# Causal attention with a gated sign network: half of the probability transposes by VectorE and SBUF-to-SBUF transfers, and the values' products ahead of the scores

## The chip, the cores and the metric

The kernel runs on one core of a Trainium2 chip. The metric is device microseconds of one execution, from start to end. The program is written with named engines: PE (TensorE, matmuls), DVE (VectorE), ACT (ScalarE), POOL (GpSimd) and SP (SyncE, which here only issues DMAs). Everything is fp32.

## The reference

```python
# x: (4, 512, 1024)
m = jnp.mean(x, -1, keepdims=True); v = jnp.var(x, -1, keepdims=True)
xn = (x - m) / jnp.sqrt(v + eps)
# attention, 16 heads of 64, rotary on q and k, causal
q, k, v = (split_heads(xn @ W) for W in (Wq, Wk, Wv))
p = softmax(mask(rotary(q) @ rotary(k).T / 8))
s = merge_heads(p @ v) @ Wo
# gate: a network with the signs of its weights and per-token channel scales
r = softmax(xn @ gate_w.T)                   # 8 experts
y = (xn * (r @ in_scale)) @ sign(weight).T
g = silu(y * (r @ out_scale) + bias)
return x + s * g
```

The listing is abridged. What matters for the change is the product of the softmax's probabilities with the values. The scores of a 512 x 512 head lie with queries on partitions, so that the row maximum and sum run along the free dimension. The product with V needs keys on partitions. So every probability block of 128 x 128 that the causal mask leaves (10 of 16 per head) must be transposed in between: 4 batches x 16 heads x 10 = 640 blocks.

## The kernel before, in words

**Units, groups, slots.** A *unit* `(b, g, i)` is a pair of heads, 2 x 64 rows on 128 partitions. A *group* `(b, g)` is two units, four heads; there are 16 groups. The main loop (from L879) has one *slot* per group. In the slot of group k, PE computes the projections of group k. Three weight blocks (q, k and a half of v's) make 84 steps, most of them one step of a Strassen scheme with matmuls of 128 x 256 (`project_qk` L330, matmul L342; `project_v` L410, matmul L429). Among these steps lie the attention *pieces* of groups before: scores of group k-1 and values of group k-2, which are called the "late" units, `w` (unit 0) and `v` (unit 1).

**The order.** PE's order is written by hand: `manual_schedule(engines={PE})` (L70) makes PE run in program order. `attention_pieces` (L839) gives a list of closures, and `interleave` (L870) spreads the projection steps evenly behind them. The other engines are ordered by the framework's scheduler, which moves instructions among each other as it expects them to become ready, except those wrapped in `keep_in_program_order`. The built program's order on each engine is fixed before the run.

**The pieces before.** Sixteen of them: five banks of transposes of `w`; block 1's scores of both units and `values(w)`; five banks of transposes of `v`; block 3's scores of both units and `values(v)`; nothing; blocks 2 and 0 of both units (`scores_02`); nothing; nothing. Some slots add to these: the router (`router` L617, a new batch's routing matmuls), loads, the sign weights, and in the slots with g > 1 the next batch's layernorm (`layernorm` L198, which is called ahead of the slot's pieces, L914 and L915) and the transposes of its normalized x (`transpose_x`).

**Scores.** `scores` (L512) takes a list of blocks. Block i is 128 queries of two heads against the (i+1) x 128 keys that the mask leaves. It has two matmuls on PE (L517), mask add and row maximum on DVE (L528, L532), two exponentials with row sums on ACT (L535), the reciprocal on DVE (L543) and two scalings on POOL (L545), in place in the probability tile. The scores lie in PSUM in the pool `ps_sc`: two buffers of two banks each. A buffer is free for PE again once the exponentials have read it. Probability tiles were three tags in the pool `probs`: block 1 (3 buffers), block 3 (2), blocks 0 and 2 together (2).

**Transposes.** `transpose_p` (L577) puts up to four 128 x 128 transposes by PE (L583) into one bank of the four-bank PSUM `ring`, which the projections use too, and copies the bank into the tile `pT` (one buffer), by DVE (L587) or by ACT (L589) in turn. `values` (L591) runs eight matmuls (L599) from `pT` into one bank, copies the result over V's tile by DVE (L608) and stores it to the HBM array `at_d` (L609, SP's queue).

**Other work that the prediction's steps name.** `form_w` (L296) and `form_x` are DVE's sums of Strassen's quarters of the weights and of x. `rotary` has four ACT copies of 32 partitions (L323, L324), one DVE product and two POOL operations (L326, L327) per unit and per q or k. Weight loads are SP DMAs of 1 MB, issued by `load_w` (L245) for a pool of three buffers. `rt_d` takes the router's result, 16 KB per store.

**The tail.** After the last slot come the last group's scores, three units' transposes and values, the gate (`dense` takes steps of the sign network's matmuls as fill) and the output projection. Before, the order from L1058 is: transposes of `w`, `split(0, 0)`, `scores_1`, `split(0, 1)`, `values(w)`, then transposes of `v` with `dense` between them, `scores_3`, `values(v)`, `dense`, ..., `scores_02`.

Of the kernel before, what the change touches and what calls it, by code (L numbers as in the profile page):

```python
# [21 lines left out]
H, D = 16, 64  # L22
# [13 lines left out]

T_BANKS = [
    [(0, 0, i) for i in range(4)],
    [(1, 0, i) for i in range(4)],
    [(0, 1, 1), (0, 1, 2), (0, 1, 3), (0, 3, 3)],  # L40
    [(1, 1, 1), (1, 1, 2), (1, 1, 3), (1, 3, 3)],
    [(0, 2, 2), (0, 2, 3), (1, 2, 2), (1, 2, 3)],
]


def t_place(h, j):

    return [(h, 0), (2 + h, 0), (4, 256 * h), (2 + h, 384)][j]
# [3 lines left out]
def attn_gated_ffn_kernel(  # L52
# [453 lines left out]
    def probs(u, i):  # L506

        if i % 2:
            return PR[u, i]
        return PR[u, 0][:, :, P * i // 2 : P * i // 2 + (i + 1) * P]  # L510
# [42 lines left out]
    def new_probs(u, n, cols, bufs):  # L553
        PR[u, n] = pp.tile(
            [P, 2, cols], F32, tag=f"p{n}", name="p%d_%d_%d_%d" % (n, *u), bufs=bufs
        )

    def scores_1(units):
        ps = sc_bank(units[0], 1)
        for u in units:  # L560
            new_probs(u, 1, 2 * P, 3)
        scores([(u, 1, ps[:, :, n * TH : (n + 1) * TH]) for n, u in enumerate(units)])

    def scores_3(units):
        for u in units:
            new_probs(u, 3, S, 2)
        scores([(u, 3, sc_bank(u, 3)) for u in units])

    def scores_02(units):
        blocks = []  # L570
        for u in units:
            new_probs(u, 0, S, 2)
            ps = sc_bank(u, 0)
            blocks += [(u, 2, ps[:, :, P:]), (u, 0, ps[:, :, :P])]
        scores(blocks)

    def transpose_p(u, n):  # L577
        un = "%d_%d_%d" % u
        if u not in PT:
            PT[u] = ptp.tile([P, 5, S], F32, tag="pT", name=f"pT_{un}")  # L580
        tp = tp_bank(f"ptp_{un}_{n}")
        for k, (h, j, i) in enumerate(T_BANKS[n]):
            nc.tensor.transpose(tp[:, k, :], probs(u, i)[:, h, j * P : (j + 1) * P], ident)  # L583
        dst = PT[u][:, n, :]
        src = tp.rearrange("p j q -> p (j q)")
        if n % 2:
            nc.vector.tensor_copy(dst, src)  # L587
        else:
            nc.scalar.copy(dst, src)  # L589

    def values(u):  # L591
        b, g, i = u
        pr = g + NGRP * i
        pv = bank("pv_%d_%d_%d" % u)
        for j in range(TPB):
            for h in range(2):
                r = h * D
                n, o = t_place(h, j)
                nc.tensor.matmul(  # L599
                    pv[r : r + D, j * P :],  # L600
                    lhsT=V[u][:, j, r : r + D],
                    rhs=PT[u][:, n, o : o + (TPB - j) * P],
# [4 lines left out]
        at = V[u].rearrange("p t c -> p (t c)")  # L607
        nc.vector.tensor_copy(at, pv)  # L608
        nc.sync.dma_start(  # L609
            out=at_d[b].rearrange("t p (c q) -> p t c q", c=NC)[:, :, pr, :],  # L610
            in_=at.rearrange("p (t q) -> p t q", t=TPB),
# [227 lines left out]
    def attention_pieces(k, late):  # L839
# [4 lines left out]
        def pt(u):  # L844
            return [lambda n=n: transpose_p(u, n) for n in range(5)] if u else []

        def with_values(scores_of, u):
            def both():
                scores_of(units)
                if u:  # L850
                    values(u)

            return both

        def wait():
            pass

        pieces = [
            *pt(w),
            with_values(scores_1, w),  # L860
            *pt(v),
            with_values(scores_3, v),
            wait,
            lambda: scores_02(units),
            wait,
            wait,
        ]
# [11 lines left out]
    for k, (b, g) in enumerate(groups):  # L879
# [4 lines left out]
        if g == 0:  # L884
# [14 lines left out]
            else:  # L899

                if b < B - 1:
                    pieces.insert(7, routing[0])
                pieces.insert(10, routing[1])
# [518 lines left out]
```

## Time and profile before

| | |
|---|---|
| median of 3 runs | 1169.93 us (1169.38 to 1170.2) |
| profiled execution, its own time | 1170.42 us |
| its span, first to last instruction | 1168.6 us |
| mean granted TensorE clock | 0.998 |
| PE busy (matmul) | 1159.0 us, 99%, 5816 instructions |
| DVE busy | 826.0 us, 71%, 1452 instructions |
| ACT busy | 496.8 us, 43%, 1132 instructions |
| POOL busy | 559.8 us, 48%, 590 instructions |
| DMA | 121.92 MB, mean 104 GB/s |

All of this comes from one profiled execution. Its own time is 1.8 us above its span: the rest lies before the first and after the last instruction. A group of instructions is written with its line, its engine, output <- input by the program's names and the tile's size; then a count, busy time, mean duration, and the idle time of the engine just before these instructions with the one that ended it. Matmuls are pipelined: one starts before the other has ended, so that busy sums and means of PE say less than the distance from start to start. In the order in time, each line gives the start in us, the duration, the engine, the line and the operation; several alike are joined to one line with their count. A bracket at the end tells an idle time before and who ended it.

A batch of four slots takes some 209 us, so a slot some 52 us, and DVE is busy 34 to 41 us of each.

### The profile page before, as it was taken

What the parts mean: (1) busy time and instruction counts of PE and PEld (TensorE: products, weight loads), DVE (VectorE), ACT (ScalarE), POOL (GpSimd) and SP (SyncE); (2) the same over time, 40 slices, a digit from 0 to 9 for tenths busy, and PEclk for the clock granted to TensorE, in tenths of its full rate; (3) what the DMA queues carried; (4) which work ended last, traced back from release to release, by engine and by line L of the source; (5) the groups of instructions that cost most, each with busy time, mean ns of one, the idle gap of its engine ahead of it and who ended that gap; (6) DMA issues with size and microseconds to landing.
All of it is one profiled execution on the core that took longest, in us unless ns stands there. A gap on an engine that the chain in (4) does not pass through costs nothing.

```text
span 1168.6 us, 16127 instructions
## 1 busy us (share of the span) xinstructions
PE 1159.0 (99%) x5816; PEld 851.2 (73%) x5816; DVE 826.0 (71%) x1452; ACT 496.8 (43%) x1132; POOL 559.8 (48%) x590
## 2 busy tenths in 40 slices
PE   9999999999999999999999999999999999999998
PEld 8887787878778787877878787877775455545554
DVE  7866686677767667776867776675768786677664
ACT  2552664354356444534743563364442131223121
POOL 0661554355246435623642654264465554454435
PEclk9999999999999999999999999999999999999999
DMA  8412522322242141223236221220603424332331
GB/s 311 134 37 90 162 82 67 133 84 82 81 132 103 54 153 50 98 100 118 81 91 226 84 73 58 78 82 14 216 15 108 130 95 145 112 95 100 135 108 54
DMA packets 62319, 121.92 MB, mean 104 GB/s; under 512 B 5280, under 2 KB 40864, under 8 KB 56224
## 3 DMA queue, kind: packets, MB, share of 16 engines
q1 hardware_dynamic: 57376, 112.11, 28.6%
q0 software_dynamic: 4576, 8.39, 2.1%
q8 instruction: 46, 0.75, 0.2%
q10 hardware_dynamic: 288, 0.39, 0.1%
q14 instruction: 33, 0.27, 0.1%
HBM read 95.45 MB, written 25.43 MB: 103 GB/s over the span
## 4 chain that ended last, share of the span: by engine, by line
PE 92%; DVE 3%; ACT 2%; issue 1%; POOL 1%; POOLq 0%; DVEq 0%; ACTq 0%
PE pj L342 31%; PE wo L1243 15%; PE pj L429 15%; PE ff L1183 7%; PE pv L599 6%; PE sc L517 6%; PE ptp L583 6%; PE ff L1004 3%; PE xtp L210 1%; ACT p L535 1%; PE idle L793 1%; DVE S L296 1%; PE lg L622 1%; DVE w L296 1%; ACT sw L324 1%
## 5 line engine op out<-in xcount | busy, mean ns | idle before, releaser
L545 POOL TENSOR_SCALAR p<-p,rs 128x128 f32<-128x128 f32 (+3 forms) x256 | 171.2, 682 | 265.6 <-DVE rs L543 265.5
L535 ACT ACTIVATE p<-sc,nmx 128x128 f32<-128x128 f32 (+3 forms) x256 | 132.7, 524 | 158.9 <-DVE nmx L532 151.4
L342 PE MATMUL pj<-X,w 128*128 128x256 f32 x576 | 138.3, 381 | 0.2 <-ACT X L216 0.2
L326 POOL TENSOR_TENSOR sw<-sw,sin_sb 128x512 f32<-128x512 f32 x64 | 87.5, 1367 | 94.8 <-ACT sw L324 79.0
L342 PE MATMUL pj<-T,S 128*128 128x256 f32 x512 | 123.4, 382 | 0.1
L342 PEld LDWEIGHTS pj<-X,w 128*128 128x128 f32 x576 | 105.1, 190 | 14.4 <-issue 1.8
L342 PE MATMUL pj<-T,w 128*128 128x256 f32 x448 | 107.6, 381 | 0.0
L589 ACT COPY pT<-ptp 128x512 f32<-128x512 f32 x96 | 56.2, 586 | 120.3 <-PE ptp L583 119.9
L532 DVE TENSOR_REDUCE nmx<-sc 128x2 f32<-128x512 f32 (+3 forms) x128 | 103.7, 821 | 2.9
L342 PEld LDWEIGHTS pj<-T,S 128*128 128x128 f32 x512 | 93.3, 190 | 13.0 <-issue 0.4
L429 PE MATMUL pj<-w,X 128*128 128x256 f32 x416 | 99.6, 386 | 2.6 <-DVE w L296 2.6
L327 POOL TENSOR_TENSOR rot<-rot,sw 128x512 f32<-128x512 f32 x64 | 93.7, 1464 | 4.7
L583 PE MATMUL ptp<-ident,p 128*128 128x128 f32 x640 | 94.8, 273 | 0.3 <-ACT pT L589 0.3
L323 ACT ACTIVATE sw<-c 32x512 f32<-32x512 f32 x128 | 80.4, 628 | 34.6 <-DVE c L356 32.6
L583 PEld LDWEIGHTS ptp<-ident,p 128*128 128x128 f32 x640 | 79.0, 141 | 16.5 <-DVE pT L587 0.9
L342 PEld LDWEIGHTS pj<-T,w 128*128 128x128 f32 x448 | 82.1, 190 | 11.4 <-issue 1.8
L429 PEld LDWEIGHTS pj<-w,X 128*128 128x128 f32 x416 | 77.7, 193 | 14.0 <-DVE w L296 3.0
L517 PE MATMUL sc<-rot,rot 64*128 64x384 f32 (+3 forms) x512 | 82.0, 449 | 0.0
L429 PE MATMUL pj<-w,T 128*128 128x256 f32 x352 | 81.8, 383 | 0.0
L324 ACT ACTIVATE sw<-c 32x512 f32<-32x512 f32 x128 | 80.4, 628 | 1.7
L599 PE MATMUL pv<-pT,v 128*64 128x256 f32 (+3 forms) x512 | 76.0, 439 | 0.0
L528 DVE TENSOR_TENSOR sc<-sc,mask 128x256 f32<-128x256 f32 x128 | 53.8, 420 | 28.7 <-PE sc L517 28.4
(180 smaller groups left out, 2086.5 us busy)
## 6 DMA issues: line engine op xcount, KB each, us to landing
w<-in_wqk SPq DMA_DIRECT2D x31, 1024.0 KB, 5.2
w<-in_wv SPq DMA_DIRECT2D x16, 1024.0 KB, 4.8
x<-in_x SPq DMA_DIRECT2D x16, 512.0 KB, 3.7
xn_d<-X SPq DMA_DIRECT2D x16, 512.0 KB, 5.8
at_d<-v SPq DMA_DIRECT2D x32, 256.0 KB, 2.3
xp<-xn_d SPq DMA_DIRECT2D x16, 512.0 KB, 4.8
ap<-at_d SPq DMA_DIRECT2D x16, 512.0 KB, 4.9
xr<-in_x SPq DMA_DIRECT2D x32, 256.0 KB, 2.8
```

The source lines that it names most:

```text
L324: nc.scalar.activation(sw[r + 32 : r + 64, :], c[r : r + 32, :], AF.Copy, scale=sc)
L326: nc.gpsimd.tensor_tensor(sw, sw, sin_sb, op=ALU.mult)
L327: nc.gpsimd.tensor_tensor(rot, rot, sw, op=ALU.add)
L342: nc.tensor.matmul(ps, lhsT=wq[:, k, :], rhs=xq[:, k, :], start=(k == 0), stop=(k == 3))
L429: nc.tensor.matmul(ps[:, j, :], lhsT=xq[:, k, j * P : (j + 1) * P], rhs=wq[:, k, :], start=(k == 0), stop=(k == 3),)
L517: nc.tensor.matmul(ps[:, h, :], lhsT=Q[u][r : r + D, i * P : (i + 1) * P], rhs=K[u][r : r + D, : (i + 1) * P], start=True, stop=True,)
L532: nc.vector.tensor_reduce(nmx, ps, AX.X, ALU.max, negate=True)
L535: nc.scalar.activation(pt[:, h, :], ps[:, h, :], AF.Exp, bias=nmx[:, h : h + 1], accum_out=ssum[:, h : h + 1],)
L545: nc.gpsimd.tensor_scalar(pt[:, h, :], pt[:, h, :], rs[:, h : h + 1], 1.0, op0=ALU.mult, op1=ALU.mult,)
L583: nc.tensor.transpose(tp[:, k, :], probs(u, i)[:, h, j * P : (j + 1) * P], ident)
L599: nc.tensor.matmul(pv[r : r + D, j * P :], lhsT=V[u][:, j, r : r + D], rhs=PT[u][:, n, o : o + (TPB - j) * P], start=(j == 0), stop=(j == ...
L1243: nc.tensor.matmul(ps, lhsT=lhs[:, k, :], rhs=rhs[:, k, :], start=(first and k == 0), stop=(k == 3), skip_group_check=not first,)
```

## The change: what it does

**Layout.** The five banks of transposed blocks become one layout by *place*: a transposed tile is 4 places of 640 columns, place a holding the 32 queries of each block with (query mod 128) // 32 = a. `by_place` is that view. `OFF` holds the column at which the blocks of keys j begin (divided by places), `T_BANKS` lists blocks with offsets. One probability tile per unit, `[P, 2, 10 P]` (tag "p", 2 buffers), replaces the three tags; `QCOL` holds each block's first column.

**Unit 0 by blocks of 32.** `transpose_blocks(u)` runs 10 DVE `transpose` instructions, each of 128 partitions x 2 heads x 4 blocks x 32 columns, which transpose 32 x 32 blocks in place on their partitions, into `y`, a tile of the tag `pT`. They are pinned in program order. Then 16 DMAs on SP's queue, each of 32 partitions x 640 elements (80 KB), move the quarter of partitions a, place b, to the quarter b, place a, from SBUF to SBUF. The order is diagonal: the four of a round touch four different source and four different target quarters. The target is the unit's own probability tile. This is piece 15 of 16, and only for unit 0 of groups 0 to 13. Unit 1, and both units of groups 14 and 15, are transposed by PE as before, with copies that write runs of 32 elements (`transpose_p`); bank 4's copy falls in two.

**Order of the pieces.** Pieces 5 to 7 are now the transposes of `v`; piece 8 the values of both late units and then `scores_1`; piece 10 is `scores_023(u0)`, blocks 3, 2 and 0 of unit 0; piece 12 is `scores_023(u1)`; piece 15 is `transpose_blocks(u0)`. The other pieces are empty, but for what a slot inserts.

**Smaller parts.** The values' copy goes from DVE to ACT, with strided operands, and the values' matmuls read and write with strides of places. The router's three pieces go to places 1, 2 and 3. Layernorm of the two tiles goes into the inserted pieces, each just ahead of its own transposes of x. The split of the output scales moves to place 1. An empty piece at the end of long slots goes. In the tail, both late units' transposes and values come ahead of the scores, and the scores there are `scores_1`, `scores_023(u0)`, `scores_023(u1)`.

```diff
 T_BANKS = [
-    [(0, 0, i) for i in range(4)],
-    [(1, 0, i) for i in range(4)],
-    [(0, 1, 1), (0, 1, 2), (0, 1, 3), (0, 3, 3)],
-    [(1, 1, 1), (1, 1, 2), (1, 1, 3), (1, 3, 3)],
-    [(0, 2, 2), (0, 2, 3), (1, 2, 2), (1, 2, 3)],
+    [(0, 0, [(0, i) for i in range(4)])],
+    [(1, 0, [(0, i) for i in range(4)])],
+    [(0, OFF[1], [(1, 1), (1, 2), (1, 3), (3, 3)])],
+    [(1, OFF[1], [(1, 1), (1, 2), (1, 3), (3, 3)])],
+    [(h, OFF[2], [(2, 2), (2, 3)]) for h in range(2)],
 ]
...
+    def new_probs(u):
+        PR[u] = pp.tile([P, 2, 10 * P], F32, tag="p", name="p_%d_%d_%d" % u)
...
+    def scores_023(u):
+        ps = sc_bank(u, 0)
+        scores([(u, 3, sc_bank(u, 3)), (u, 2, ps[:, :, P:]), (u, 0, ps[:, :, :P])])
+
+    def by_place(t):
+        return t.rearrange("p (a n) -> p a n", a=4)
+
+    def transpose_blocks(u):
+        y = ptp.tile([P, 20 * P], F32, tag="pT", name="y_%d_%d_%d" % u)
+        out = by_place(y).rearrange("p b (h n) -> p h b n", h=2)
+        for j in range(TPB):
+            for i in range(j, TPB):
+                src = probs(u, i)[:, :, j * P : (j + 1) * P]
+                o = OFF[j] + 32 * (i - j)
+                tc.keep_in_program_order(
+                    nc.vector.transpose(
+                        out[:, :, :, o : o + 32], src.rearrange("p h (b c) -> p h b c", b=4)
+                    )
+                )
+        PT[u] = by_place(PR[u].rearrange("p h n -> p (h n)"))
+        for n in range(4):
+            for a in range(4):
+                b = (a + n) % 4
+                nc.sync.dma_start(
+                    out=PT[u][32 * b : 32 * b + 32, a, :],
+                    in_=by_place(y)[32 * a : 32 * a + 32, b, :],
+                )
...
-        at = V[u].rearrange("p t c -> p (t c)")
-        nc.vector.tensor_copy(at, pv)
+        at = V[u]
+        nc.scalar.copy(
+            at.rearrange("p t (a q) -> p t a q", q=32), pv.rearrange("p a (t q) -> p t a q", q=32)
+        )
...
-        pieces = [
-            *pt(w),
-            with_values(scores_1, w),
-            *pt(v),
-            with_values(scores_3, v),
-            wait,
-            lambda: scores_02(units),
-            wait,
-            wait,
-        ]
+        u0, u1 = units
+        pieces = [nothing] * 16
+        if w:
+            pieces[5] = lambda: [transpose_p(v, n) for n in (0, 1)]
+            pieces[6] = lambda: [transpose_p(v, n) for n in (2, 3)]
+            pieces[7] = lambda: transpose_p(v, 4)
+        pieces[8] = both_values if w else lambda: scores_1(units)
+        pieces[10] = lambda: scores_023(u0)
+        pieces[12] = lambda: scores_023(u1)
+        if k < len(groups) - 2:
+            pieces[15] = lambda: transpose_blocks(u0)
...
             t0 = 2 * (g - 2)
+            extra = [lambda: layernorm(b + 1, t0)]
             for t in range(t0, t0 + 2):
-                layernorm(b + 1, t)
-            extra = [
-                lambda t=t, h=h: transpose_x(b + 1, t, h) for t in range(t0, t0 + 2) for h in range(2)
-            ]
+                extra.append(lambda t=t: transpose_x(b + 1, t, 0))
+                if t == t0:
+                    extra.append(lambda: layernorm(b + 1, t0 + 1))
+                extra.append(lambda t=t: transpose_x(b + 1, t, 1))
...
-        if len(pieces) > 18:
-            pieces.append(lambda: None)
```

## The prediction, made before the change was run

> **What bounds the kernel now.** I read the busy shares first, then the chain of work that ended last, then the groups, then the order in time of one stretch.
>
> ```profile
> PE 1159.0 (99%) x5816; PEld 851.2 (73%) x5816; DVE 826.0 (71%) x1452; ACT 496.8 (43%) x1132; POOL 559.8 (48%) x590
> ...
> PE 92%; DVE 3%; ACT 2%; issue 1%; POOL 1%; POOLq 0%; DVEq 0%; ACTq 0%
> PE pj L342 31%; PE wo L1243 15%; PE pj L429 15%; PE ff L1183 7%; PE pv L599 6%; PE sc L517 6%; PE ptp L583 6%; PE ff L1004 3%; PE xtp L210 1%; ACT p L535 1%; PE idle L793 1%; DVE S L296 1%; PE lg L622 1%; DVE w L296 1%; ACT sw L324 1%
> ...
> L583 PE MATMUL ptp<-ident,p 128*128 128x128 f32 x640 | 94.8, 273 | 0.3 <-ACT pT L589 0.3
> L587 DVE COPY pT<-ptp 128x512 f32<-128x512 f32 x64 | 43.7, 684 | 18.8 <-PE ptp L583 18.7
> ```
>
> PE is busy almost without a gap and carries 92% of the chain, so what leaves PE comes off the end unless PE then waits. The 640 probability transposes (`ptp`, L583) hold 6% of the chain, about 70 us. Neither the busy sum (94.8 us) nor the mean (273 ns) is their price, since PE overlaps instructions; the price is start to start:
>
> ```profile
> 443.99 0.60 PE L583 MATMUL ptp<-ident,p 128*128 128x128 f32 x4
> 444.42 1.89 PE L342 MATMUL pj<-T,w 128*128 128x256 f32 x8
> 446.15 0.60 PE L583 MATMUL ptp<-ident,p 128*128 128x128 f32 x4
> ...
> 450.25 1.99 PE L517 MATMUL sc<-rot,rot 64*128 64x512 f32 x8
> 452.17 2.38 PE L599 MATMUL pv<-pT,v 128*64 128x512 f32 x16
> ...
> 458.55 2.00 PE L517 MATMUL sc<-rot,rot 64*128 64x384 f32 x16
> ```
>
> Four transposes take 0.43 us, 0.108 each (640 of them: 69 us, the 6%). Eight rows of a projection, which are four steps of the program, take 1.73 us: 0.432 a step. The last three lines show the other fact that matters: block 3's scores of both units start at 450.25 and their two score banks are wanted again at 458.55, 8.3 us later. The same stretch on VectorE:
>
> ```profile
> 451.43 0.43 DVE L528 TENSOR_TENSOR sc<-sc,mask 128x256 f32<-128x256 f32 x1
> 451.89 1.22 DVE L532 TENSOR_REDUCE nmx<-sc 128x2 f32<-128x1024 f32 x1
> 453.04 0.42 DVE L528 TENSOR_TENSOR sc<-sc,mask 128x256 f32<-128x256 f32 x1
> 453.49 1.23 DVE L532 TENSOR_REDUCE nmx<-sc 128x2 f32<-128x1024 f32 x1
> ...
> 457.55 0.17 DVE L543 RECIPROCAL rs<-ssum 128x2 f32<-128x2 f32 x1 [0.58 <-ACT p L535]
> ```
>
> The last exponential is done when the reciprocal starts, 457.55: a margin of one microsecond in 8.3. In time order I find no PE gap over 0.3 us between 101 and 830 us. PE runs without waits because the scores are this far apart.
>
> [...] here, on SP's queue and into HBM, 256 KB (`at_d`) land in 2.3 us, 16 KB (`rt_d`) in 2.2.
>
> **The change part by part.** *Removed from PE*: unit 0 of 14 of the 16 groups, 14 x 20 = 280 transposes x 0.108 = 30.3 us. *Removed with them*: per unit two VectorE copies (0.68 each) and three ScalarE copies (0.59).
>
> *Added on VectorE*: 10 block transposes per unit of 256 elements per partition. The nearest row is a 256-element VectorE operation here, 0.41 to 0.42 us[...]. I take 0.37: 3.7 us per unit in one block. [...] Net per slot of 52 us: +3.7, -1.4 (copies), -1.4 (`values` copies both units on ScalarE) = +0.9 on an engine busy 36 to 41 us. Hidden as a sum. Queued behind the block are one projection's evictions and, at a batch's end, `form_x`. By the built order I follow VectorE past it: at a batch's end T3 is ready some 2 us before PE wants it, with the router's 1.9 us as cover, so nothing. The block waits for POOL's last scaling of unit 0, done some 5 us before it.
>
> *Added on SP*: 16 transfers of 80 KB per unit at 0.33 to 0.43 us of issue (rows of L253, L667) = 5.3 to 6.9 us, landing 2.3 us after the last. Weight loads (5.2 us to land) queue behind; by the built order those behind are first read 15 us or more after, so nothing; with that cover gone, up to 6 us each. The buffer y is the one that unit 1's PE transposes are copied into next, so those copies wait for the transfers. From the end of a slot: block done at 1 to 4 us, transfers landed at 10 to 12; first copy wanted at 10.4 (group 3) to 14. ScalarE and VectorE may stand 1.5 us in group 3, and four PSUM banks of the ring cover that. The PV matmuls of unit 0 want the data at about 18 us: nothing.
>
> *Moved: the scores.* This is where the gain can go. Now block 1 of both units, all of unit 0 and all of unit 1 are three groups, two or three pieces apart, over the same two banks: block 1's bank is taken by unit 0's blocks 2 and 0, and that by unit 1's. I step through a slot with group 0, with spacings from the trace; zero is PE's start on block 3 of unit 0. PE: block 3 to 0.96, blocks 2 and 0 to 1.93, ten steps x 0.432 to 6.25, block 3 of unit 1 to 7.2, then it wants the bank of unit 0's blocks 2 and 0. VectorE: mask and maximum of block 3 (0.45 + 1.15) from 1.16 to 2.8, of block 2 (0.45 + 0.87) to 4.1, then by the built order an eviction, a weight form, two rotary products and three reciprocals among the mask and maximum of block 0, to 7.4. ScalarE: exponentials of block 3 (1.4) to 4.3, of block 2 (1.15) to 5.5, four rotary copies of 0.64 to 8.06, block 0 (0.75) to 8.85. So PE waits about 1.7 us. Without the four copies VectorE's chain alone gives 8.2, a wait of 1.0. The same stepping gives 1.4 for group 2, and 2.6 to 2.8 for groups 1 and 3, where layernorm now lies among the scores, with table switches of 1.28 us before and after its square root (27 switches in the built program for 15), and block 1's bank is late too.
>
> Over 15 slots: floor 15 x 1.0 = 15 us; all as stepped about 30. I take 20 (1.3 a slot): above the floor, since ScalarE's copies do lie there, and below the stepping, because layernorm's statistics need only x and may have run before the window in the half of the slots that cost most. *Moved: the tail.* Two times PE now goes from transposes straight to PV with only their copies between: about 1.1 + 0.6 us against the 0.6 seen there before, +1.1. PE's strided operands in PV and the strided copies (runs of 32 elements): taken as nothing; 0 to 0.1 us for each of 32 units and 150 copies, hidden on the copies.
>
> Sum against the profiled execution, 1170.42 us (span 1168.6): 1170.4 - 30.3 + 20 + 1.1 = 1161.2. The median of the runs is 0.5 lower: 1161.
>
> **Rivals.** *All given back.* Every slot waits as stepped: 30 us, plus the tail's 1.1: 1171. For it: the 1.0 us margin of before and the fixed queue orders. Against it: the uncertain start of layernorm's part. *Slower: the packed scores overrun.* VectorE falls behind in the half slot of scores; place: `scores_023` of unit 1, price: each further 0.7 us of lateness per slot 10 us. It decides from 2.0 us per slot on; at 2.6 in all, 39 us, the end is at 1180. For it: weight forms of VectorE average 0.77 us where I stepped with 0.65, through POOL. Against it: VectorE has 11 to 16 idle us per slot. *Slower: slow block transposes*, 0.65 us each: block 2.8 us later, y free at 13 to 15 us, past the cover of the ring, about 1.5 us in 14 slots: 1161 + 21 = 1182. *No gain because the transposes were hidden*: excluded, as PE is the chain.
>
> **How the numbers follow.** Forecast, faster: 0.50 (its own range 1150 to 1167; 1150 leaves 9 us of waits). All given back: 0.18, of which 0.11 within 0.2%, which is 2.3 us and about what can be told from no change, and 0.07 above. Overrun 0.20, slow transposes 0.12. So faster 0.50, same 0.11, slower 0.39. Range: 1150 to 1183.
>
> **What would show it.** Right: PE `ptp` x360; VectorE transposes near 0.37 us; PE waits at L514 for ScalarE's exponentials (L532) of 1 to 1.5 us per slot; PE busy falls by more than the span does. Wrong: waits of over 2 us per slot at L514, PE idle at L600 behind the transfers, or weight loads late behind them.

## The result, and the profile after

The changed kernel takes 1285.13 us (median of 4 runs, 1281.83 to 1287.46), the kernel before 1169.66 us in the same runs: 1.0986 times as long, 95% interval [1.0964, 1.1008]. It is 115.5 us slower. The prediction said 1161, with a range that ended at 1183.

The page of the changed kernel (profiled execution 1285.98 us, span 1284.3 us) gives, line by line, the busy engines, the granted clock of PE in 40 slices, the chain that ended last, the transposes and the transfers.

```profile
PE 1170.8 (91%) x5536; PEld 844.1 (66%) x5536; DVE 847.2 (66%) x1532; ACT 509.3 (40%) x1152; POOL 550.1 (43%) x590
...
PEclk9998999999989899999989889999999999999999
...
PE 55%; DVE 17%; ACT 15%; issue 5%; POOL 3%; SPq 3%; DMA 2%; POOLq 0%; ACTq 0%; DVEq 0%
...
L600 PE MATMUL ptp<-ident,p 128*128 128x128 f32 x360 | 59.5, 295 | 57.5 <-ACT pT L609 50.4
...
p<-y SPq DMA_DIRECT2D x224, 80.0 KB, 2.1
```

The 280 transposes did leave PE. But PE now carries 55% of the chain that ended last in place of 92%, and 5536 matmuls keep it busy for 11.8 us *longer* than 5816 did. So the growth of the span, 115.7 us, has three terms: 113.5 us without work on PE against 9.6 before (+103.9), 30.3 us of transposes gone, and some 42 us by which the other matmuls are busy longer (1170.8 - 1159.0 + 30.3). The 42 is what is left over, so that the sum closes proves nothing about it. The row of the clock says where part of it comes from: six slices with an 8, where before every slice had a 9 (a slice is 32 us). The mean clock is 0.970; as the clock's records in this trace have only 1.00 and 0.50, that is 76 us at half clock. PE was busy in 62 of them, which accounts for 31 of the 42 us (before: 2). The other 13 or so fit the number of stops, as the runs on bank 4 show below.

What PE waited for in the changed kernel (the view of waits: total us, times, longest):

```profile
PE ptp L600 <- ACT pT L609: 50.4, 29, 5.4
PE sc L514 <- ACT p L532: 24.8, 18, 2.4
PE pj L341 <- DVE T L314: 8.1, 1, 8.1
PE os L797 <- ACT p L532: 4.2, 1, 4.2
PE ptp L600 <- DVE c L392: 4.0, 2, 2.0
PE rt L684 <- DVE rex L680: 3.9, 3, 1.4
```

Half of PE's idle time stands at the transposes of unit 1 that PE kept, for the copies of their banks. (All lines with `ptp` add up to 57.6 us; the expectations below speak of 69, which is too high.) The second line is the wait that the prediction feared. In the order of time, PE in one slot (its projection begins at 99.34):

```profile
111.00 1.04 PE L600 MATMUL ptp<-ident,p 128*128 128x128 f32 x8
...
114.90 0.60 PE L600 MATMUL ptp<-ident,p 128*128 128x128 f32 x4
120.87 1.11 PE L600 MATMUL ptp<-ident,p 128*128 128x128 f32 x4 [5.37 <-ACT pT L609]
121.78 2.77 PE L341 MATMUL pj<-X,w 128*128 128x256 f32 x6
124.34 1.06 PE L341 MATMUL pj<-T,S 128*128 128x256 f32 x2
```

The first bank is full at 111.6, and the fourth group of transposes can't begin before it is copied out: a stop of 5.4 us. ScalarE, meanwhile:

```profile
110.38 0.37 ACT L390 COPY part<-pj 128x256 f32<-128x256 f32 x1 [6.94 <-PE pj L341]
113.47 0.63 ACT L322 ACTIVATE sw<-c 32x512 f32<-32x512 f32 x1 [2.71 <-DVE c L355]
...
117.33 1.28 ACT L187 ACT_TABLE_LOAD   x1
118.62 0.29 ACT L187 ACTIVATE std<-mv,eps 128x1 f32<-128x1 f32 x1
...
120.23 1.07 ACT L609 COPY pT<-ptp 128x512 f32<-128x512 f32 x2
```

It idled from 110.75 to 113.47, then ran eight rotary copies and layernorm's square root, and only then the two copies. Their banks were full by 115.5, and the buffer was free by then too (next lines). They stood last because the scheduler had put them there. The transfers on SP's queue:

```profile
100.26 10.64 SPq L586 DMA_DIRECT2D p<-y  x16
111.00 1.40 SPq L252 DMA_DIRECT2D w<-in_wqk  x1
```

Sixteen issues took 10.6 us, 0.66 each, and with 2.1 us to landing the buffer was free at about 113, 13.7 us into the slot. What followed the stop is in the view by stretches. After the stretch and its length it has the busy us of PE, weight load, DVE, ACT and POOL with counts, then PE's clock, the DMA share and GB/s:

```profile
121.00:122.00 1.00, 1.00 (x5) 1.00 (x6) 0.00 (x0) 0.31 (x1) 0.92 (x2) 0.50 0.00 0
...
124.00:125.00 1.00, 1.00 (x4) 0.81 (x3) 0.00 (x0) 0.36 (x1) 0.00 (x0) 0.50 0.00 0
...
127.00:128.00 1.00, 1.00 (x6) 0.90 (x5) 0.00 (x0) 0.14 (x1) 0.00 (x0) 1.00 0.00 0
```

For five microseconds after the stop PE ran at half its clock. From 121.78 the six projection matmuls take 2.56 us to the start of the next, where 1.30 is their pace.

### The profile page after: what moved, and what is told of

Same layout as the page of the kernel before. It is cut to its first block, busy times and chain, and to the rows that moved or that the text cites. A ratio compares the mean times of both kernels' runs of the same rounds, so it can differ in the third digit from the quotient of the medians.

```text
span 1284.3 us, 16115 instructions
## 1 busy us (share of the span) xinstructions
PE 1170.8 (91%) x5536; PEld 844.1 (66%) x5536; DVE 847.2 (66%) x1532; ACT 509.3 (40%) x1152; POOL 550.1 (43%) x590
## 4 chain that ended last, share of the span: by engine, by line
PE 55%; DVE 17%; ACT 15%; issue 5%; POOL 3%; SPq 3%; DMA 2%; POOLq 0%; ACTq 0%; DVEq 0%
PE pj L341 13%; PE wo L1255 13%; PE pj L428 8%; PE ff L1195 6%; PE pv L619 5%; ACT p L532 4%; ACT sw L322 3%; ACT sw L323 3%; PE sc L514 3%; DVE nmx L529 3%; PE ptp L600 2%; SPq L586 2%; DVE S L295 2%; DVE y L576 2%; PE ff L1017 2%
## 5 line engine op out<-in xcount | busy, mean ns | idle before, releaser
L542 POOL TENSOR_SCALAR p<-p,rs 128x512 f32<-128x512 f32 (+3 forms) x256 | 160.2, 640 | 307.3 <-DVE rs L540 286.9
L532 ACT ACTIVATE p<-sc,nmx 128x512 f32<-128x512 f32 (+3 forms) x256 | 132.6, 525 | 139.0 <-DVE nmx L529 122.1
L514 PE MATMUL sc<-rot,rot 64*128 64x384 f32 (+3 forms) x512 | 92.4, 476 | 25.3 <-ACT p L532 24.8
L341 PEld LDWEIGHTS pj<-T,S 128*128 128x128 f32 x512 | 99.2, 198 | 24.6 <-DVE T L314 8.5
L600 PE MATMUL ptp<-ident,p 128*128 128x128 f32 x360 | 59.5, 295 | 57.5 <-ACT pT L609 50.4
L428 PE MATMUL pj<-w,X 128*128 128x256 f32 x416 | 106.1, 404 | 0.7 <-DVE X L213 0.7
L529 DVE TENSOR_REDUCE nmx<-sc 128x2 f32<-128x768 f32 (+3 forms) x128 | 104.9, 820 | 2.7
L514 PEld LDWEIGHTS sc<-rot,rot 64*128 64x128 f32 x512 | 45.2, 194 | 73.2 <-ACT p L532 47.3
L600 PEld LDWEIGHTS ptp<-ident,p 128*128 128x128 f32 x360 | 44.8, 150 | 72.5 <-ACT pT L609 58.0
L391 POOL TENSOR_TENSOR part<-part,part 128x256 f32<-128x256 f32 x32 | 25.0, 782 | 138.2 <-ACT part L390 135.6
```

The source lines that it names most:

```text
L341: nc.tensor.matmul(ps, lhsT=wq[:, k, :], rhs=xq[:, k, :], start=(k == 0), stop=(k == 3))
L428: nc.tensor.matmul(ps[:, j, :], lhsT=xq[:, k, j * P : (j + 1) * P], rhs=wq[:, k, :], start=(k == 0), stop=(k == 3),)
L514: nc.tensor.matmul(ps[:, h, :], lhsT=Q[u][r : r + D, i * P : (i + 1) * P], rhs=K[u][r : r + D, : (i + 1) * P], start=True, stop=True,)
L529: nc.vector.tensor_reduce(nmx, ps, AX.X, ALU.max, negate=True)
L532: nc.scalar.activation(pt[:, h, :], ps[:, h, :], AF.Exp, bias=nmx[:, h : h + 1], accum_out=ssum[:, h : h + 1],)
L542: nc.gpsimd.tensor_scalar(pt[:, h, :], pt[:, h, :], rs[:, h : h + 1], 1.0, op0=ALU.mult, op1=ALU.mult,)
```

## The experiments

### Undo one part

Four runs each undo one part of the change. Theory A says that the transfers cost most, by the buffer that they share with unit 1's copies. Its rivals are layernorm's table loads in ScalarE's queue (B) and the packed scores.

**All by PE.** Unit 0 goes back to PE, the new order stays.

```diff
         if w:
+            pieces[0] = lambda: [transpose_p(w, n) for n in (0, 1)]
+            pieces[1] = lambda: [transpose_p(w, n) for n in (2, 3)]
+            pieces[2] = lambda: transpose_p(w, 4)
+            pieces[3] = lambda: values(w)
...
-        if k < len(groups) - 2:
-            pieces[15] = lambda: transpose_blocks(u0)
```

> Unit 0 of every group goes back to PE's transposes (280 more, 30.3 us of PE), at pieces 0 to 2, with its values at piece 3; the new order of the scores, the layernorm in pieces, the new layout and the strided copies stay. No VectorE transposes, no transfers. Theory A, that the transfers (their buffer, which unit 1's copies need, and their place in SP's queue) cost most of the loss: the 69 us of waits at the transposes, the 8 us wait at the last batch's form of x and most of the half-clock stretches go, 30 come back, so about 1213 us, with 20 to 25 us of waits at the scores left. Rival B, that layernorm's square root and its table loads in ScalarE's queue hold the copies: the waits at the transposes stay, at least in the slots with layernorm, and the time is 1270 or more.

Measured: 1266.7 us, only 18 less, where 1213 was expected. With no transfer and no VectorE transpose left, PE still waited 38.9 us at the transposes. So neither theory was the whole of it. The trace showed a new place, between the two pairs of bank 4:

```profile
119.04 0.38 PE L600 MATMUL ptp<-ident,p 128*128 128x128 f32 x2
121.78 0.69 PE L600 MATMUL ptp<-ident,p 128*128 128x128 f32 x2 [2.36 <-ACT pT L609]
```

The changed `transpose_p` issues two transposes, their half copy, two transposes, their half copy. The second pair writes the bank that the first copy reads, and waits for it: PE stands in the middle of one bank for whatever is queued on ScalarE (here three rotary copies and an eviction, until 121.36). All 32 of this run's stops for ScalarE's copies are of this kind.

**Own buffer.** The block transposes write a tile of their own.

```diff
-        y = ptp.tile([P, 20 * P], F32, tag="pT", name="y_%d_%d_%d" % u)
+        y = ptp.tile([P, 20 * P], F32, tag="y", name="y_%d_%d_%d" % u)
```

> The block transposes write a tile of their own (tag y), so that the copies of unit 1's PE transposes no longer wait for the transfers to have read it. To make room for 10 KB per partition, sign block 6 lies in block 5's tile and the output scales in the input scales' tile, so that the gate is computed with wrong values; the work is the same. Theory A, the shared buffer: the copies stand on ScalarE ahead of the rotary copies again, the waits at the transposes (69 us) and the half-clock stretches behind them go, about 1210 us; the scores' waits (25 us) and the 8 us at the last batch's form of x stay. Rival B, layernorm: less than 15 us are saved, 1270 or more.

This kernel, and the three below that are built on it (own buffer with bank 4 first, and the two combined ones), leave out the tile of one sign block and that of the output scales. Measured: 1251.7 us (1246 to 1260), 33 less in place of 75. The first copy now stands on ScalarE just behind its bank, ahead of the rotary copies:

```profile
109.56 0.59 ACT L610 COPY pT<-ptp 128x512 f32<-128x512 f32 x1 [0.88 <-PE ptp L601]
111.39 0.63 ACT L323 ACTIVATE sw<-c 32x512 f32<-32x512 f32 x1 [1.25 <-DVE c L356]
```

That is A's mechanism: it is the shared buffer that moved the copies back in the fixed order. What stayed were 33.4 us of waits for ScalarE's copies, nearly all of it (28.7 us, 18 stops) in bank 4, up to 3.5 us each.

**Layernorm back.** Layernorm of both tiles is called ahead of the slot's pieces again.

```diff
-            extra = [lambda: layernorm(b + 1, t0)]
+            extra = []
             for t in range(t0, t0 + 2):
+                layernorm(b + 1, t)
```

> Layernorm of both tiles is called ahead of the slot's pieces again, as in the kernel before; all else as changed. Theory A: the table load and the square root leave the stretch in which the copies stand (1.6 us in 6 slots, 10 us), but the copies still stand behind eight rotary copies and the transfers, so about 1270 us. Rival B: the waits at the transposes fall from 69 to under 25 us, about 1235.

Measured: 1278.3 us, 7 less. The waits at the transposes stay, 46.7 us of 50.4, so rival B falls as the main cause. But the waits at the scores fell from 24.8 to 15.0 us: layernorm's place made some 10 of those. New waits at the transposes of x (6.2 us in place of 0.3 for layernorm's last step) took part of the gain back.

**Scores by block.**

```diff
-        pieces[10] = lambda: scores_023(u0)
-        pieces[12] = lambda: scores_023(u1)
+        pieces[10] = lambda: scores_3(units)
+        pieces[13] = lambda: scores_02(units)
```

> The scores go by block again: block 1 of both units at piece 8, block 3 of both at piece 10, blocks 2 and 0 of both at piece 13; the transposes stay at piece 15, all else as changed. If the waits at the scores come from the packed order by unit, as predicted, they fall from 25 us to under 5: about 1262 us. Rival: the two score buffers are late whatever the order, because the scores now have half a slot: the waits stay, 1280 or more.

Measured: 1270.0 us. The waits at the scores fell to 4.3 us, 20 less as expected, but the time by only 15 in place of 23. Waits for VectorE came back in their place: the router's went from 3.9 to 8.7 us, those for an eviction (`c`) from 4.0 to 9.4 at the transposes of unit 1 and from 1.6 to 8.2 at those of x.

### Bank 4 in two halves

**Bank 4 first.** In the changed kernel all four transposes come ahead of the two half copies.

```diff
                 k += 1
+        k = 0
+        for h, o, blocks in T_BANKS[n]:
+            first, k = k, k + len(blocks)
             o += 320 * h
```

> In the changed kernel, bank 4's four transposes all come ahead of its two half copies; nothing else changes. All-by-PE showed PE standing between the two pairs of transposes of bank 4, until the first half copy has come up in ScalarE's queue. Theory C, that the copy in two halves stalls PE: the changed kernel has 18 such stops (14 in the slots, 4 in the tail) of 0.6 to 1.6 us, 15 us, and some half-clock time behind them, so about 1267 us. Rival: PE only waits later for the same copies, at the values' products, and the time stays within 5 us of 1285.

**The kernel before, with only bank 4's copy in halves.**

```diff
-        for k, (h, j, i) in enumerate(T_BANKS[n]):
-            nc.tensor.transpose(tp[:, k, :], probs(u, i)[:, h, j * P : (j + 1) * P], ident)
+        parts = ((0, 2), (2, 4)) if n == 4 else ((0, 4),)
+        for a, z in parts:
+            for k in range(a, z):
+                h, j, i = T_BANKS[n][k]
+                nc.tensor.transpose(tp[:, k, :], probs(u, i)[:, h, j * P : (j + 1) * P], ident)
```

> The kernel before with one edit: bank 4's copy falls in two halves, each issued behind its own pair of transposes, as in the changed kernel. Theory C: the second pair waits for the first half's copy, 32 times; with the mean of all-by-PE, 1.4 us a stop, 43 us, so about 1213 us. Rival: in the old order of pieces ScalarE comes to the copy at once, and a stop is only the copy's own latency, 0.5 us: 1186.

Measured: 1275.9 us for the first, 9 us less (18 were expected, or under 5); 1193.2 us for the second, 1.020 times before [1.0185, 1.0215]. The waits of the second:

```profile
PE ptp L586 <- ACT pT L592: 15.8, 32, 1.5
```

These are 32 stops, one for each unit. In the old order a stop is half a microsecond of waiting, as the rival said. In the new order it is longer, 1.2 us in all by PE (38.9 us in 32), because more stands ahead of the half copy. The time grew by more than the waits, 24 us: PE's busy time rose too, from 1159.0 to 1165.5 us, with the clock at 0.999. So a stop costs another 0.2 us without any loss of clock. The changed kernel has 70 stops of PE over 0.15 us, against 5 before: at 0.2 us each that is about the 13 us which the clock leaves open (an estimate from these two runs).

**The same edit without the shared buffer.** In all by PE, and in own buffer:

> All units by PE in the new order of pieces, as in the run of that name, and bank 4's transposes ahead of its half copies: what is left against the kernel before is the new order alone. In the all-by-PE run PE stood at the second pair of bank 4 for most of the 43 us that it waited at transposes, since the first half copy lay in ScalarE's queue behind rotary copies. If those stops only wait for the copy, about 1220 us. Rival, as for the same edit in the changed kernel (9 us): PE meets the same late copies at the values or at the ring's banks: 1250 or more.

> The changed kernel with a buffer of its own for the block transposes (sign block 6 in block 5's tile and the output scales in the input scales' tile, so that the gate is computed with wrong values) and bank 4's transposes ahead of its half copies: it differs from all by PE with the same edit only in that unit 0 goes by VectorE and transfers, without the shared buffer. If this path pays its 30 us, it lies 20 to 30 us under that run; if its work on VectorE and on SP's queue comes back as waits of PE, within 10 us of it or above. From the own-buffer run (1252) and 15 us for bank 4: about 1237 us.

Measured: 1212.0 us (from 1266.7) and 1207.4 us (from 1251.7). The halves cost 55 and 44 us there, but only 9 where the shared buffer already stops PE for the same queue. (The second was expected at 1237, with too small a price for bank 4.) The largest waits that are left, first in all by PE:

```profile
PE sc L514 <- ACT p L532: 20.0, 15, 2.4
```

and with unit 0 by VectorE and a buffer of its own:

```profile
PE sc L515 <- ACT p L533: 24.8, 18, 2.4
PE pj L342 <- DVE T L315: 8.0, 1, 8.0
PE ptp L601 <- DVE c L393: 3.9, 2, 2.0
PE rt L688 <- DVE rex L684: 3.8, 3, 1.4
PE pj L342 <- DVE part L356: 3.6, 3, 1.2
PE ptp L601 <- ACT pT L613: 2.7, 3, 1.3
```

These two runs differ in the path of unit 0, and in the two tiles that the second leaves out. It takes 30.3 us off PE and ends 4.7 us ahead. The two runs' waits show where 25 of the 30 went: the form of x behind the store and the transfers 8.0, the scores 4.8, the transposes 6.3 (6.6, where all by PE has 0.3), the router 3.8, the projections' evictions 2.5 (3.6 less 1.1).

The runs make a stair from before to the changed kernel: new order and layout 1169.7 to 1212.0 (+42), path of unit 0 to 1207.4 (-5), the shared buffer to 1275.9 (+68), bank 4's halves to 1285.1 (+9). The last two depend on which is taken first: the other way round the halves cost 44 and the shared buffer 33. At the step of +68 the waits at the transposes for copies of their banks went from 2.7 to 45.1 us, and the time at half clock from 34 to 80 us. The two tiles left out have no part in it that shows: behind the last projection the two runs take 346.8 and 347.1 us, so that the step lies in the slots.

### Is it the order by unit, or the room?

**The kernel before, with scores by unit**, and **with layernorm in pieces too**.

```diff
-            with_values(scores_3, v),
+            lambda: (values(v) if v else None, scores_023(units[0])),
             wait,
-            lambda: scores_02(units),
+            lambda: scores_023(units[1]),
```

> The kernel before with one edit: piece 11 has the values of unit 1 and then blocks 3, 2 and 0 of unit 0, and piece 13 blocks 3, 2 and 0 of unit 1, so that unit 1's scores come two pieces behind unit 0's, as in the changed kernel. If the score buffers are what waits there, PE stands 1.0 to 2.5 us a slot for ScalarE's exponentials, 15 slots, some 24 us as in the changed kernel: about 1195 us. Rival: the waits of the changed kernel come from the table loads of layernorm and the rotary copies in that half slot: under 8 us here, 1177.

> The kernel before with the scores by unit (that alone: 1177 us, 3 us of waits at the scores) and with layernorm of the two tiles in the inserted pieces, each ahead of its own transposes of x, as changed. If layernorm among the scores makes the waits there (table loads in ScalarE's queue between exponentials), they come to 12 us or more and the time to about 1190 us. Rival: under 1181 us, and the changed kernel's 25 us at the scores have another source.

Measured: 1176.5 us and 1177.4 us, 1.0059 [1.0044, 1.0074] and 1.0067 [1.005, 1.0084]. Waits at the scores in the first:

```profile
PE sc L517 <- ACT p L535: 2.6, 6, 0.6
```

So in the old room neither the order by unit nor layernorm makes long waits. Here block 1's scores stand six pieces ahead of unit 0's; in the changed kernel, two. There each of them counts: the scores by block took 20 of the 24.8 us away, and layernorm back took 10. So the likely cause is the room, three groups over two score buffers within four pieces, with layernorm's table switches (1.28 us each, 27 in place of 15) on top; no run changed the room alone.

### The smaller places

**Tail: unit 0's scores after 3 steps of the gate in place of 6**, and **the last store of x from ScalarE's queue**.

```diff
-    dense(gates, 6)
+    dense(gates, 3)
     scores_023(u0)
-    dense(gates, 6)
+    dense(gates, 9)
```

> The changed kernel, with scores_023 of unit 0 in the tail behind 3 steps of the gate in place of 6, and 9 steps behind it in place of 6: the score banks that out_scales takes next come free earlier. The tail of the changed kernel is 11 us longer than before. If that is the wait at out_scales (4.2 us) and the half clock behind it (3.5 us), about 1277 us. Rival: the wait moves to the scores of unit 0 or to the steps, and the time stays within 3 us of 1285.

```diff
-            nc.sync.dma_start(
+            (nc.scalar if (b, t) == (B - 1, TPB - 1) else nc.sync).dma_start(
                 out=xn_d[b, t]
```

> The changed kernel, with the last store of x of the last batch issued on ScalarE's queue in place of SP's, where it lies behind 16 transfers. If SP's queue made the 8 us stop of PE ahead of the last batch's Strassen forms, the stop goes: about 1276 us. Rival: the store lands as late for another reason (VectorE and its own landing of about 4 us): under 4 us are saved.

Measured: 1280.3 and 1278.0 us, 5 and 7 less (ratios to before 1.0942 [1.0926, 1.0958] and 1.0921 [1.0904, 1.0939], to be set beside 1.0986). In the first the wait of 4.2 us at `os` (the output scales' banks) fell to 0.3. In the second the stop of 8.1 us went, and 2.5 us came back at the router. In the changed kernel the store stands behind 16 transfers, and the first form of the last batch, which writes over x in place, waits for its landing:

```profile
699.04 10.70 SPq L586 DMA_DIRECT2D p<-y  x16
709.84 0.57 SPq L217 DMA_DIRECT2D xn_d<-X  x1
```

```profile
713.55 1.23 DVE L314 TENSOR_TENSOR X<-X 128x1024 f32<-128x1024 f32 x1 [4.08 <-DMA xn_d<-X]
```

### Put together

**Combined**, twice: the edits own buffer, bank 4 first, scores by block and the store, and the router at its old places, with layernorm ahead of the slot, then in pieces.

```diff
-                pieces[3], pieces[2] = routing[2], routing[1]
                 if b < B - 1:
-                    pieces[1] = routing[0]
+                    pieces.insert(7, routing[0])
+                pieces.insert(10, routing[1])
+                pieces.insert(13, routing[2])
```

> The changed kernel with a buffer of its own for the block transposes (with sign block 6 in block 5's tile and the output scales in the input scales' tile, so that the gate is computed with wrong values), bank 4's transposes ahead of its half copies, the scores by block, layernorm ahead of the slot, the router at the places of before and the last batch's last store of x on ScalarE's queue. If the causes add up (69 us at the transposes, 20 at the scores, 8 at the store, 4 at the router, and some 25 us of half clock behind them), about 1160 us, faster than before. Rival: each freed wait uncovers the next, a queue order of ScalarE: more than 1200.

> The combined kernel (own buffer, with the same wrong values in the gate; bank 4's transposes first; scores by block; router at the places of before; the last batch's last store of x on ScalarE's queue) with layernorm in the inserted pieces, as changed, in place of ahead of the slot. There PE stood 22 us at the transposes of x for layernorm's last step on VectorE, behind the block transposes. If that wait was layernorm's place, about 1193 us with under 5 us left of it. Rival: the table loads come back among the scores and copies: 1210 or more.

Measured: 1214.2 and 1189.7 us. In the first PE waited 22.6 us at the transposes of x for layernorm's last step on VectorE, behind the block transposes; the second took 16 of them away. The first was expected at 1160. So the causes add up but for 54 us with layernorm ahead of the slot, and but for some 30 with layernorm in pieces.

**In place, with the whole computation.** Unit 1's probability tile is 13 blocks wide, block (i, j) at i + 3j, so that the transposed blocks of one j lie side by side and each PE bank is copied back over its own source. Then the tag `pT` belongs to the block transposes (and the last two groups) alone, and nothing of the computation is left out. The scores by block, the router's places, the store and the tail are as in the runs above.

```diff
+            if n < 2:
+                dst, src = PR[u][:, n, : 4 * P], tp.rearrange("p k q -> p (k q)")
...
-                    rhs=PT[u][:, :, o : o + 32 * (TPB - j)],
+                        PR[u][:, h, 4 * j * P : (3 * j + TPB) * P]
...
-            pieces.insert(8, lambda: make_sign(n + 1))
-            pieces.insert(4, lambda: make_sign(n))
+            pieces.insert(15, lambda: make_sign(n + 1))
+            pieces.insert(11, lambda: make_sign(n))
```

> A version with the whole computation: unit 1's probability tile is laid out so that each bank of PE's transposes is copied back over its own source blocks (13 blocks wide in place of 10), so that the block transposes have the tag pT to themselves; unit 1's copies and values are plain again; scores by block; router at the places of before; the last store on ScalarE's queue; the tail with unit 0's scores after 3 steps; the sign weights made from piece 11 on. If the causes found add up: combined with layernorm in pieces gave 1190; the tail's 8 us and 10 us of stops at the transposes behind the sign weights go: about 1172 us, between 1163 and 1185. Rival: in-place copies tie the banks together and PE stops at them: 1195 or more.

The three runs after it each add one edit: the order of the pools and of the two probability tiles (with the input scales at piece 5 in place of 3), layernorm first, the sums later.

```diff
-    pp = right(name="probs", bufs=2)
     ptp = right(name="probsT", bufs=1)
+    pp = right(name="probs", bufs=2)
...
-                pieces.insert(3, lambda: in_scales(g - 1, score_banks))
+                pieces.insert(5, lambda: in_scales(g - 1, score_banks))
```

> The in-place version (whole computation), with three stops taken out that its trace showed: the tile of unit 1's probabilities now lies where the output projection's first sums don't go (those waited 4.5 us for its last values, and PE ran at half clock behind), the pool of the transposed blocks is allocated ahead of the probabilities', and the input scales' banks are asked for two pieces later (2.9 us). Expected: 1180 less 7 less 3, about 1170 us, between 1165 and 1176; the bet is open whether it beats the kernel before (1170).

```diff
-            extra = [lambda: layernorm(b + 1, t0)]
+            extra = [lambda t=t: layernorm(b + 1, t) for t in (t0, t0 + 1)]
```

> The same, with layernorm of both tiles in the first two inserted pieces, ahead of all four transposes of x, in place of each just ahead of its own two. PE stood 6.9 us at the transposes of x for layernorm's last step, with half clock behind it: if the room of two more pieces covers that, 8 us under the run without this edit, about 1162 us. Rival: the earlier table loads land among the copies of unit 1's transposes and give it back: no difference beyond 3 us.

```diff
-    for c in range(4):
-        sum_wo(4, c)
...
                 form_a(q, n)
+        if q == 0:
+            for c in range(4):
+                sum_wo(4, c)
```

> The in-place version with layernorm first (1175), with the last four of the output projection's sums (sum_wo of t4) behind the first forms of the values in place of ahead of them. The trace of that run still had PE waiting 4.5 us for the form S, and half clock behind it; S lay on VectorE behind those four sums (2.5 us), not behind the memory that the earlier repair moved. Expected: 2.5 us and some of the half clock, about 1171 us, no clear difference from the kernel before. Rival: the sums are then late themselves: 1175 or more.

Measured: 1180.5, 1179.3, 1175.2 and 1173.9 us. The repaired memory places did nothing: PE waited for the form S as long as before, 4.5 us, so that part of its expectation was wrong. The wait of 2.9 us for the input scales did go, with no clear gain. Layernorm first took 4 of the 8 expected us. The last is 1.0038 times before [1.0024, 1.0052]: 111 us of the loss are undone, and it is still 4 us slower. Its busy engines and largest waits:

```profile
PE 1135.0 (97%) x5536; PEld 823.0 (70%) x5536; DVE 855.3 (73%) x1532; ACT 499.0 (43%) x1130; POOL 556.2 (47%) x590
```

```profile
PE pj L348 <- DVE c L399: 5.3, 3, 3.8
PE ptp L622 <- DVE c L399: 3.6, 2, 1.9
PE ptp L622 <- DVE part L362: 3.2, 4, 1.1
PE ptp L622 <- ACT p L638: 3.1, 3, 1.3
```

PE is busy 24 us less than before and idle 27 us more, in many small stops of which most wait for VectorE. No single wait is over 5.3 us in total.

## Why the prediction was wrong, step by step

The sum had -30 us for unit 0's path, +21 for the new order and the tail, and nothing for the rest. The stair has -5, +42, and +77 or so for two things that the sum put at nothing: the shared buffer and bank 4's halves. Step by step:

1. **Removed from PE, 30.3 us: right.** 280 transposes went. Between all by PE and own buffer, both with bank 4 first, PE's busy time falls by 29.7 us (1175.9 to 1146.2).
2. **VectorE's block transposes: right.** 0.37 us each was taken, the author's estimate, a little under the one row of 256 elements that the trace before showed (0.41 to 0.42). Ten take 3.38 us (0.34), and each by itself took 395 to 436 ns, close to that row. The rival's 0.65 us had no measured row behind it; it falls.
3. **"ScalarE and VectorE may stand 1.5 us in group 3, and four PSUM banks of the ring cover that": the step that failed, +68 us (33 without bank 4 mended).** The landing was only a little late (13.7 us into the slot, where 10 to 12 was said). What failed was to price the shared buffer by its landing time alone. On an engine with a fixed order, a wait that the scheduler expects also changes where an instruction stands in the queue: in the slot shown the first copy starts at 120.23 us, with a buffer of its own at 109.56. The copies came to stand behind eight rotary copies and a table load, and PE, at the fourth bank, behind them. The prediction used the built order in other places; here it counted when the buffer came free, and not what ScalarE runs first.
4. **"The strided copies ... taken as nothing": wrong, +9 us here, 44 to 55 without the shared buffer.** The strides cost nothing that shows: ScalarE's copy of a whole bank has a median of 587 ns (before 586), and the values' matmuls of PE have the same median of 432 ns. What cost is that one bank's copy fell in two, with PE's transposes between. The change was read for the copies' length, not for PE's order against them.
5. **The moved scores, 20 us: right in kind and size.** It has 24.8 us in 18 waits at L514, all for ScalarE's exponentials, and the stepping had the pattern: in the slots of groups 1 and 3, where it put layernorm's table switches, PE waits 1.9 to 2.6 us (in the three batches that have a next one), with group 2 only 0.7. Layernorm back took 10 us off, mostly in those slots, so that part is borne out too. In the old room it doesn't show (1176.5 and 1177.4 us without and with layernorm in pieces).
6. **SP's queue, "nothing": wrong, +7 us.** An issue takes 0.63 to 0.67 us in 13 of the 14 groups of sixteen (0.73 in the other), not 0.33 to 0.43. The weight loads behind did come in time. What was missed is the store of x, which in the last batch alone guards an in-place write.
7. **The tail, 1.1 us: wrong, +11** (from the last projection's end to the end 348.3 us against 337.4). The wait of 4.2 us for the score banks at the output scales is shown (5 us came back without it, the loss of pace behind it included); the rest isn't taken apart.
8. **Not in the sum at all: what a stop costs beyond its length.** Some 42 us of the loss are matmuls that are busy longer: 31 at half clock, the rest in line with 0.2 us a stop. Behind the long stop, 5.4 us of idle, the clock was 0.50 for five us; behind one of 1.9 us in all by PE with bank 4 first it fell to half as well, as the last section shows. A wait of PE was priced by its length; each us of new idle time came with 0.4 us more of busy time (42 on 104).

The rival "slower: the packed scores overrun" had its wait where it said, though not at its price. The weight forms did take longer beside POOL: before, one of 128x512 took 0.69 us with POOL idle throughout (median of 70) and 0.77 with POOL busy throughout (median of 31, the longest 1.64). The rival in which y comes free past the ring's cover had the right place by luck: its reason was slow transposes, and they were fast. What stopped PE there was SP's issues a little, and the order of ScalarE's queue.

## What to carry to other kernels

When a change lets two uses share a buffer, read in the built program where the waiting instruction now stands on its engine and what stands ahead of it; the wait itself may be the smaller part. A bank that several instructions fill should be filled before the first copy out of it is issued, or the filling engine waits in the middle (15.8 us in 32 stops where the kernel before had its bank 4 in halves). On an engine that is busy 99%, price each new stop with the pace that is lost behind it (here 42 us on 104 of idle time), and don't take a saving of 3% as one before every queue between has been walked through: here 30 us off PE were worth 5 even with the worst two faults gone.

## What the runs showed of the hardware

**PE's clock changed on a grid of 3.41 us.** In all by PE with bank 4 first, PE stood 1.9 us at the scores, until 194.12, and the clock fell to half. In the changed kernel a stop of the same place and length, until 209.47, left the clock at 1.00. What differs is how the stop lies. In the trace of the changed kernel all 33 changes of the clock lie on a grid with steps of 3.413 us, within 1 ns, and in that of the kernel before so do its three. Here are the two stops with the edges of each run's grid as stretches (the columns are those of the first section's view), first all by PE with bank 4 first, then the changed kernel:

```profile
190.77:194.18 3.41, 1.49 (x8) 0.36 (x6) 3.37 (x10) 1.57 (x7) 3.02 (x4) 1.00 0.84 282
194.18:197.60 3.42, 3.42 (x12) 2.33 (x13) 3.06 (x6) 1.45 (x4) 0.72 (x2) 0.50 0.04 12
```

```profile
204.71:208.13 3.42, 2.84 (x13) 1.52 (x11) 3.39 (x9) 2.17 (x7) 2.33 (x3) 1.00 0.49 153
208.13:211.54 3.41, 2.07 (x13) 1.59 (x14) 3.01 (x8) 0.81 (x4) 1.73 (x4) 1.00 0.52 156
```

The first stop lies within one stretch, and PE is busy in 1.49 of its 3.41 us (44%), as the view counts it. The second is cut by an edge, and leaves 83% and 61%. In the two traces of before and after, each of the 19 changes from full to half clock came behind a stretch with PE busy for 0 to 46%. Of the 672 stretches at full clock that were followed by full clock, two were busy for 44 and 45%, all others for 53% or more. The 17 changes back came behind stretches that were 80 to 100% busy at half clock, though one of 85% was followed by half clock again. So one stop of 1.9 us, within one stretch, cost the clock, and one cut by an edge did not. Behind the stop of 5.4 us in the first section the half clock lasted two such steps, from 119.38 to 126.21.

**A small transfer held the queue longer than a large load.** In the changed kernel a transfer from SBUF to SBUF of 32 partitions x 2560 bytes landed in 2.1 us, but held SP's queue for 0.66 us (sixteen in 10.64; the issue's own row has a median of 0.59). The issue of a weight load of 1 MB has a median of 0.35 to 0.37 us there, though single ones take longer, such as the 1.40 above, and of 0.33 in the kernel before.
